# Channel mix of seven batches beside the last ticks of the second attention, and the slots' norms at later steps of the first

## The chip, the cores and the metric

The kernel runs on one core of a Trainium2 chip, as one program with one launch. The metric is the device time of one execution in microseconds (us). The engines are TensorE (PE: matmuls and transposes; its weight loads are listed as PEld), VectorE (DVE), ScalarE (ACT), GpSimd (POOL) and SyncE (SP), which issues most of the DMAs. Each engine has its own queue and takes its instructions in order; semaphores connect them.

## The reference, cut to what matters

Two layers, each an attention and a feed-forward part, over `x` of 8 batches x 256 tokens x 256 channels in float32, with a context of 8 x 256 x 192:

```python
x = x + L0_xattn(layernorm(x), ctx, mask)   # 16 heads of 16
x = x + L0_ffn(layernorm(x))                # soft mixture of 8 experts, 128 slots each
x = x + L1_xattn(layernorm(x), ctx)         # 16 heads of 64, output bias
x = x + L1_ffn(layernorm(x))                # channel mix
```

The edit touches two pieces of it. The first is the norm of the experts' slots, computed once: `sn = slots / max(|slots|, 1e-12) * 16 * gamma`, with 8 x 128 slots of 256 channels. The second is the channel mix of the last line, per batch:

```python
x_prev = concat([zeros, x[:, :-1]], axis=1)      # the token before
xr = mu_r * x + (1 - mu_r) * x_prev
xk = mu_k * x + (1 - mu_k) * x_prev
out = sigmoid(xr @ W_r.T) * (relu(xk @ W_k.T) ** 2 @ W_v.T)
```

## The kernel before, in words

All activations stay on the chip: `x_sb` holds the 16 tiles of 128 tokens (two a batch). Everything is float32. A scheduler places instructions by data dependences and may take them out of the written order, except those wrapped in `tc.keep_in_program_order`; after that every engine's queue is fixed.

**First attention** (spans about 5 to 275 us). A loop over 76 steps `h`: each does the scores of a quarter-batch twice, once by query for the row maxima (`NM`, DVE reductions, line 486) and, six steps later, once by key for the exponentials (ACT, line 497). The scores go to two PSUM buffers (`ps_big`), and a step's scores wait until the maxima of the step before have been read from them. What else is done lies in a table written out by hand, `at(h, f)`: function `f` runs at step `h`. In it are the layer-norm statistics of tile pairs (`ln_pair`, steps 0, 1, 2 for pairs 1, 2, 3), mask rows (`key_rows`), projections, and the slots' norm in three parts: `slot_sum(e)` (a square and a sum on DVE for each of 8 experts, lines 323 and 324, steps 1 to 4), `slot_scale` (one square root on ACT and three small DVE instructions, step 5), and `slot_piece(e2)` (scaling, four transposes on PE, two DVE instructions, steps 17, 25, 33, 41). The slots (`se`, 1 MB) are loaded by SP after the other inputs. The result `snT` is first read at step 48.

**Mixture of experts** (about 275 to 912 us): PE streams the experts' matmuls. The edit doesn't touch it.

**Second attention** (about 900 to 1315 us). A software pipeline over 32 groups of two steps (a step is two heads of a batch; four groups are a batch) with five stages: 0 scores, maxima (line 1201) and exponentials (line 1206, four a step); 1 the normalisation on POOL (line 1219); 2 the transposes of the weights (`pe`) with copies `et` (line 1235, one on DVE and one on ACT); 3 values (`o`); 4 the output projection (`po`, after the last group of a batch), added to `x_sb` on DVE (line 1267). Tick `n` runs stage 3 of group n-3, the next batch's projections, stage 4 of n-4, stage 2 of n-2, stage 1 of n-1, and stage 0 of n. Batch 7 is groups 28 to 31, so batch `b` is complete in `x_sb` at tick 4b+7. At n = 20 the statistics of tiles 0 to 7 for the next part are written (`ln_half`). Its matmuls and transposes are kept in program order. The PSUM pool `mm` has three buffers, used by all projections and transposes.

**Channel mix** (about 1315 us to the end). After the attention's pools are closed, the three weights and `mu` are loaded by SP (lines 1321 to 1324). `run_pipeline` then runs three stages over the eight batches: `mix` (layer norm, four transposes `pt_xf`, a copy `yT` with a zero column ahead, and for each of r and k two ACT scalings, line 1343, and two DVE instructions, line 1346), `keys` (`pk`, relu on ACT, square on POOL, line 1369; `pr`, sigmoid on ACT, line 1382), `values` (`pv`, the product on DVE, line 1398, the add of `x_sb` on POOL, line 1399, and the store).

Of the kernel before, what the change touches and what calls it, by code (L numbers as in the profile page):

```python
# [7 lines left out]

F32 = mybir.dt.float32
U8 = mybir.dt.uint8  # L10
AF = mybir.ActivationFunctionType
ALU = mybir.AluOpType
AX = mybir.AxisListType

P = 128
# [7 lines left out]
EPS = 1e-5  # L23
# [39 lines left out]
def kernel(ctx: ExitStack, tc: tile.TileContext, a: dict, out: bass.AP):  # L63
    nc = tc.nc
# [6 lines left out]
    def matmul(out, lhsT, rhs, start, stop):  # L71

        tc.keep_in_program_order(nc.tensor.matmul(out, lhsT=lhsT, rhs=rhs, start=start, stop=stop))  # L73
# [10 lines left out]
    def ps_mm(name):  # L84
        return ps.tile([P, 512], F32, tag="mm", bufs=3, name=name)
# [23 lines left out]
            a["x"][P * n : P * (n + of), :].rearrange("(t p) d -> p t d", p=P),  # L109
        )  # L110

    def ln_half(half, name):

        mv = stat.tile([P, 8, 2], F32, tag="mv", name=f"mv_{name}")
        for i in range(8):
            st = stat.tile([P, 6], F32, tag="bst", bufs=4, name=f"bst_{name}_{i}")
            nc.vector.bn_stats(st, x_sb[:, half * 8 + i, :])
            nc.vector.bn_aggr(mv[:, i, :], st)
        rstd = stat.tile([P, 8], F32, tag="rstd", name=f"rstd_{name}")
        nc.scalar.activation(rstd, mv[:, :, 1], AF.Sqrt, bias=epsb)  # L120
        nc.vector.reciprocal(rstd, rstd)
        return mv, rstd

    def ln_tiles(n, of, name):

# [10 lines left out]
    def ln_pair(p, name):  # L136
        return ln_tiles(4 * p, 4, name)
# [85 lines left out]
    with ExitStack() as l0:  # L223
# [96 lines left out]

        def slot_sum(e):
            sq = work.tile([P, 2, D], F32, tag="xh", bufs=3, name=f"sq_{e}")
            nc.vector.tensor_tensor(sq[:, 0, :], se[:, e, :], se[:, e, :], ALU.mult)
            nc.vector.tensor_reduce(ssq[:, e : e + 1], sq[:, 0, :], AX.X, ALU.add)

        def slot_scale():

            nc.scalar.activation(ssq, ssq, AF.Sqrt)
            nc.vector.tensor_scalar(ssq, ssq, 1e-12, None, ALU.max)
            nc.vector.reciprocal(ssq, ssq)  # L330
            nc.vector.tensor_scalar(ssq, ssq, 16.0, None, ALU.mult)
# [244 lines left out]
        def at(h, f):  # L576
            whole.setdefault(h, []).append(f)
# [7 lines left out]
        queries0(0, 0)  # L585
        stats0 += [ln_tiles(2, 2, "l0_1")]
        for p in range(1, 4):
            at(p - 1, lambda p=p: stats0.extend([ln_pair(p, f"l0_{2 * p}")] * 2))
        at(0, lambda: keys0(0, 1))
        at(1, lambda: queries0(0, 1))  # L590
        at(1, lambda: tokens0(1))
# [18 lines left out]
            at(h + 25, lambda b=b: values0(b + 1))  # L610

        for e in range(E):
            at(1 + e // 2, lambda e=e: slot_sum(e))
        at(5, slot_scale)
        for g in range(3):
            at(16 * g + 28, lambda g=g: moe_mean(g))
        at(30, lambda: moe_scale([0]))
        at(63, lambda: moe_scale([1, 2]))
        for e2 in range(4):
            at(17 + 8 * e2, lambda e2=e2: slot_piece(e2))  # L620
        for b in range(B):
            for qb in range(2):
                at(8 * b + 19, lambda b=b, qb=qb: project(b, qb, tos[b]))
# [438 lines left out]
    with ExitStack() as l1:  # L1062
# [15 lines left out]
        nc.sync.dma_start(wo, a["wo1"].rearrange("(c p) f -> p c f", p=P))  # L1078
        bo = w1p.tile([P, D], F32, name="bo1")
        nc.sync.dma_start(bo, a["bo1"].partition_broadcast(P))  # L1080

        def keys(p, t2):

# [196 lines left out]
        def stage(k, n):  # L1280
            for step in groups[n] if 0 <= n < len(groups) else ():
                if k < len(step):
                    step[k]()
# [6 lines left out]
        for pieces in qs:  # L1290
            for piece in pieces:
                piece()
        for n in range(len(groups) + 4):
            b, i = n // 4 + 1, n % 4
            stage(3, n - 3)
            if b < B:
                for piece in projs[b][1][i]:
                    piece()
            stage(4, n - 4)
            stage(2, n - 2)  # L1300
            stage(1, n - 1)


            if i < 2 and n // 8 < B // 2 - 1:
                keys(n // 8 + 1, n % 8 // 4 * 2 + i)()
            elif i >= 2 and b < B:
                projs[b][2][i - 2]()()
            stage(0, n)
            if n == 20:
                ffn_stats[0] = ln_half(0, "ffn_0")  # L1310

    with ExitStack() as l1f:
        wf = l1f.enter_context(tc.tile_pool(name="wf", bufs=1))
        pf_ = l1f.enter_context(tc.tile_pool(name="pf", bufs=2))
        wts = {}
        for n in ("wrT", "wkT", "wvT"):
            wts[n] = wf.tile([P, 2, D], F32, name=f"sb_{n}")  # L1320
            nc.sync.dma_start(wts[n], a[n].rearrange("(c p) f -> p c f", p=P))
        mu = wf.tile([P, 4], F32, name="mu")
        nc.sync.dma_start(mu[:, 0:2], a["mu_r"])
        nc.sync.dma_start(mu[:, 2:4], a["mu_k"])
        omu = wf.tile([P, 4], F32, name="omu")
        nc.vector.tensor_scalar(omu, mu, -1.0, 1.0, ALU.mult, ALU.add)
        ffn_stats[1] = ln_half(1, "ffn_1")

        steps = []
        for b in range(B):  # L1330
            st = {}

            def mix(b=b, st=st):
                mv, rstd = ffn_stats[b // 4]
                pt = transposed(normed(b, mv, rstd, "ffn"), f"xf_{b}")
                yT = pf_.tile([P, 2, S + 1], F32, tag="yT", name=f"yT_{b}")
                nc.gpsimd.memset(yT[:, :, 0:1], 0.0)
                nc.vector.tensor_copy(yT[:, :, 1 : S + 1], pt)
                for k, n in enumerate(("r", "k")):
                    m = pf_.tile([P, 2, S], F32, tag=f"x{n}", name=f"x{n}_{b}")  # L1340
                    for c in range(2):
                        i = 2 * k + c
                        nc.scalar.activation(
                            m[:, c, :], yT[:, c, 1 : S + 1], AF.Copy, scale=mu[:, i : i + 1]
                        )
                        nc.vector.scalar_tensor_tensor(
                            m[:, c, :],
                            yT[:, c, 0:S],
                            omu[:, i : i + 1],
                            m[:, c, :],  # L1350
                            ALU.mult,
                            ALU.add,
                        )
                    st[n] = m

            def keys(b=b, st=st):
                pk = ps_mm(f"pk_{b}")
                for d in range(2):
                    for c in range(2):
                        nc.tensor.matmul(  # L1360
                            pk[:, d * S : (d + 1) * S],
                            lhsT=wts["wkT"][:, c, d * P : (d + 1) * P],
                            rhs=st["k"][:, c, :],
                            start=(c == 0),
                            stop=(c == 1),
                        )
                ka = pf_.tile([P, 512], F32, tag="ka", name=f"ka_{b}")
                nc.scalar.activation(ka, pk, AF.Relu)
                nc.gpsimd.tensor_tensor(ka, ka, ka, ALU.mult)
                st["ka"] = ka.rearrange("p (d n) -> p d n", d=2)  # L1370
                pr = ps_mm(f"pr_{b}")
                for t in range(2):
                    for c in range(2):
                        nc.tensor.matmul(
                            pr[:, t * D : (t + 1) * D],
                            lhsT=st["r"][:, c, t * P : (t + 1) * P],
                            rhs=wts["wrT"][:, c, :],
                            start=(c == 0),
                            stop=(c == 1),
                        )  # L1380
                r = pf_.tile([P, 512], F32, tag="rs", name=f"rs_{b}")
                nc.scalar.activation(r, pr, AF.Sigmoid)
                st["rs"] = r

            def values(b=b, st=st):
                pv = ps_mm(f"pv_{b}")
                for t in range(2):
                    for d in range(2):
                        nc.tensor.matmul(
                            pv[:, t * D : (t + 1) * D],  # L1390
                            lhsT=st["ka"][:, d, t * P : (t + 1) * P],
                            rhs=wts["wvT"][:, d, :],
                            start=(d == 0),
                            stop=(d == 1),
                        )
                y = pf_.tile([P, 2, D], F32, tag="y", name=f"y_{b}")
                yf = y.rearrange("p t d -> p (t d)")
                nc.vector.tensor_tensor(yf, pv, st["rs"], ALU.mult)
                nc.gpsimd.tensor_tensor(
                    yf, yf, x_sb[:, 2 * b : 2 * b + 2, :].rearrange("p t d -> p (t d)"), ALU.add  # L1400
                )
                nc.sync.dma_start(
                    out[S * b : S * (b + 1), :].rearrange("(t p) d -> p t d", p=P), y
                )

            steps.append([mix, keys, values])
        run_pipeline(steps)


# [60 lines left out]
```

## Time and profile before

| | |
|---|---|
| median of 3 runs | 1375.91 us (1373.8 to 1378.23) |
| the profiled execution | 1375.81 us, span 1373.9 us from first to last instruction |
| busy in the span | PE 1326.6 us (97%), DVE 575.1 (42%), ACT 578.9 (42%), POOL 194.6 (14%) |
| mean granted TensorE clock | 0.987 |
| chain that ended last | PE 84%, ACT 6%, DVE 4%, DMA 2%, issue 2%, POOL 1% |

The profile is of one execution. The page gives busy time by engine, the span in 40 slices, the chain of work that ended last (followed back from the last instruction, at each step to what released it) and the costliest groups of instructions. A timeline lists instructions by start and duration; in square brackets stands the idle time of the engine just before, and what ended it. Where a row stands for several instructions (x2, x8), its time is from the first start to the last end.

### The profile page before, as it was taken

What the parts mean: (1) busy time and instruction counts of PE and PEld (TensorE: products, weight loads), DVE (VectorE), ACT (ScalarE), POOL (GpSimd) and SP (SyncE); (2) the same over time, 40 slices, a digit from 0 to 9 for tenths busy, and PEclk for the clock granted to TensorE, in tenths of its full rate; (3) what the DMA queues carried; (4) which work ended last, traced back from release to release, by engine and by line L of the source; (5) the groups of instructions that cost most, each with busy time, mean ns of one, the idle gap of its engine ahead of it and who ended that gap; (6) DMA issues with size and microseconds to landing.
All of it is one profiled execution on the core that took longest, in us unless ns stands there. A gap on an engine that the chain in (4) does not pass through costs nothing.

```text
span 1373.9 us, 19006 instructions
## 1 busy us (share of the span) xinstructions
PE 1326.6 (97%) x7504; PEld 961.3 (70%) x7504; DVE 575.1 (42%) x1172; ACT 578.9 (42%) x1386; POOL 194.6 (14%) x149
## 2 busy tenths in 40 slices
PE   6899999899999999999999999999999999999988
PEld 3556655468678877778767888866667667577767
DVE  5777876523330233321333110025444544554544
ACT  1445444635342254522625222204544534554643
POOL 1000001101010000100001000013332332323514
PEclk9899999999999999999999999999999999999999
DMA  8000000023133323332323325340000000000011
GB/s 250 23 2 1 1 1 1 1 96 131 65 131 131 131 76 119 130 113 83 126 69 130 131 88 173 100 126 1 1 1 1 1 1 1 1 1 1 1 31 54
DMA packets 59112, 86.84 MB, mean 63 GB/s; under 512 B 3344, under 2 KB 49040, under 8 KB 59024
## 3 DMA queue, kind: packets, MB, share of 16 engines
q1 hardware_dynamic: 57440, 84.33, 18.8%
q10 hardware_dynamic: 1584, 1.31, 0.4%
q8 instruction: 59, 0.97, 0.3%
q14 instruction: 29, 0.24, 0.1%
HBM read 83.53 MB, written 2.10 MB: 62 GB/s over the span
## 4 chain that ended last, share of the span: by engine, by line
PE 84%; ACT 6%; DVE 4%; DMA 2%; issue 2%; POOL 1%; SPq 0%; POOLq 0%; ACTq 0%; DVEq 0%
PE ph L964 16%; PE pe L980 15%; PE sc L73 8%; PE q L73 6%; PE o L73 5%; PE po L73 5%; PE k L73 5%; PE pc L1006 4%; PE v L73 4%; PE pe L76 4%; PE ln L828 3%; PE pf L910 3%; ACT ex L1206 2%; PE pf L73 1%; ACT ex L497 1%
## 5 line engine op out<-in xcount | busy, mean ns | idle before, releaser
L972 ACT ACTIVATE ht<-ph,b 128x256 f32<-128x256 f32 x256 | 119.0, 473 | 372.1 <-PE ph L964 371.7
L964 PE MATMUL ph<-slots,w 128*128 128x256 f32 x1024 | 266.8, 384 | 1.1 <-ACT ht L972 0.4
L980 PE MATMUL pe<-w,ht 128*128 128x256 f32 x1024 | 263.3, 381 | 0.0
L964 PEld LDWEIGHTS ph<-slots,w 128*128 128x128 f32 x1024 | 182.4, 189 | 54.4 <-ACT ht L972 21.7
L980 PEld LDWEIGHTS pe<-w,ht 128*128 128x128 f32 x1024 | 192.0, 190 | 29.9 <-DVE slots L989 4.2
L1219 POOL TENSOR_TENSOR ex<-ex,rz 128x1024 f32<-128x1024 f32 x64 | 120.2, 1898 | 224.4 <-DVE rz L1217 219.8
L1206 ACT ACTIVATE ex<-sc,nm 128x256 f32<-128x256 f32 x256 | 117.2, 483 | 45.8 <-DVE nm L1201 44.6
L73 PE MATMUL sc<-KT,QT 17*128 17x256 f32 (+1 forms) x1024 | 105.5, 383 | 5.7 <-DVE NM L486 4.8
L497 ACT ACTIVATE ex<-sc 128x512 f32<-128x512 f32 x128 | 74.6, 596 | 84.4 <-PE sc L73 76.6
L486 DVE TENSOR_REDUCE NM<-sc 128x2 f32<-128x512 f32 x128 | 86.7, 687 | 33.0 <-PE sc L73 28.7
L989 DVE TENSOR_TENSOR slots<-pe,b 128x512 f32<-128x512 f32 x32 | 22.1, 692 | 185.0 <-PE pe L980 185.0
L73 PEld LDWEIGHTS sc<-KT,QT 17*128 17x128 f32 (+1 forms) x1024 | 78.0, 189 | 29.0 <-issue 13.3
L73 PE MATMUL q<-xT,wq 128*128 128x256 f32 x384 | 95.4, 396 | 0.9 <-ACT V L1171 0.9
L73 PEld LDWEIGHTS q<-xT,wq 128*128 128x128 f32 x384 | 71.3, 193 | 27.0 <-issue 13.3
L888 POOL TENSOR_TENSOR es<-es,zs 128x1024 f32<-128x1024 f32 x12 | 22.7, 1893 | 445.8 <-DVE zs L887 445.8
L1201 DVE TENSOR_REDUCE nm<-sc 128x4 f32<-128x1024 f32 x64 | 75.4, 1219 | 6.5 <-PE sc L73 2.8
L73 PE MATMUL po<-wo,ot 128*128 128x256 f32 x320 | 72.6, 382 | 0.0
L76 PE MATMUL pe<-ident,ex 128*128 128x128 f32 x512 | 69.9, 278 | 0.5 <-DVE xT L1121 0.4
L73 PEld LDWEIGHTS po<-wo,ot 128*128 128x128 f32 x320 | 60.1, 190 | 11.3 <-issue 3.6
L1235 ACT COPY et<-pe 128x512 f32<-128x512 f32 x64 | 37.0, 607 | 71.9 <-PE pe L76 71.5
L76 PEld LDWEIGHTS pe<-ident,ex 128*128 128x128 f32 x512 | 56.3, 140 | 14.0 <-issue 8.0
L73 PE MATMUL o<-et,V 128*64 128x256 f32 x512 | 62.8, 385 | 0.9 <-ACT ot L1254 0.9
(186 smaller groups left out, 1642.7 us busy)
## 6 DMA issues: line engine op xcount, KB each, us to landing
w<-in_w_dram SPq DMA_DIRECT2D x64, 1024.0 KB, 6.4
b<-in_b_dram SPq DMA_DIRECT2D x32, 128.0 KB, 6.7
out_dram<-y SPq DMA_DIRECT2D x8, 256.0 KB, 2.1
x_sb<-in_x_dram SPq DMA_DIRECT2D x3, 512.0 KB, 6.1
ctx0T<-in_ctxT_dram SPq DMA_DIRECT2D x4, 256.0 KB, 6.8
ctx1T<-in_ctxT_dram SPq DMA_DIRECT2D x8, 128.0 KB, 5.9
se<-in_slots_dram SPq DMA_DIRECT2D x1, 1024.0 KB, 6.0
wq<-in_wq_dram SPq DMA_DIRECT2D x1, 1024.0 KB, 4.9
```

The source lines that it names most:

```text
L73: tc.keep_in_program_order(nc.tensor.matmul(out, lhsT=lhsT, rhs=rhs, start=start, stop=stop))
L76: tc.keep_in_program_order(nc.tensor.transpose(out, in_, ident))
L486: nc.vector.tensor_reduce(NMs[(2 * b + t // 2) % 2][:, qb, t, HD0 + 1 + 64 * i : 64 * i + 64 : 32], sc[i][:, :, 0, :], AX.X, ALU.max, nega ...
L497: nc.scalar.activation(ex[:, 2 - 2 * i : 4 - 2 * i, :], sc[1 - i][:, :, 1, :], AF.Exp)
L828: nc.tensor.matmul(pl[:, m * 512 : (m + 1) * 512], lhsT=st["xnT"][:, c, t * P : (t + 1) * P], rhs=snT[:, c, m * 512 : (m + 1) * 512], star ...
L964: nc.tensor.matmul(ph, lhsT=c_["w1"][:, c, hc * P : (hc + 1) * P], rhs=slots[e][:, c * 256 : (c + 1) * 256], start=(c == 0), stop=(c == 1),)
L972: nc.scalar.activation(ht, ph, AF.Gelu, bias=b1[:, e, hc : hc + 1])
L980: nc.tensor.matmul(c_["pe"][:, b, :], lhsT=c_["ht"][hc][:, b * SL : (b + 1) * SL], rhs=c_["w2"][:, hc, :], start=(hc == 0), stop=(hc == HI ...
L1006: nc.tensor.matmul(pc[:, :D], lhsT=CT[:, bl, e, t * P : (t + 1) * P], rhs=eos[e][:, bl, :], start=(e == 0), stop=(e == E - 1),)
L1201: nc.vector.tensor_reduce(nm, sc, AX.X, ALU.max, negate=True)
L1206: nc.scalar.activation(ex[:, i, qb, :], sc[:, i, qb, :], AF.Exp, bias=nm[:, i, qb : qb + 1], accum_out=z[:, i, qb : qb + 1],)
L1219: nc.gpsimd.tensor_tensor(ex, ex, rz.rearrange("p h q -> p (h q)").unsqueeze(2).to_broadcast([P, 4, S]), ALU.mult,)
```

## The change

It does four things.

1. The first attention's table: statistics of pairs 1 to 3 at steps 1 to 3, slot sums at steps 18 to 25, `slot_scale` at step 30, `slot_piece` at steps 32, 36, 40 and 44. The square and the root are kept in program order.
2. The channel mix's weights, `mu`, `omu` and one `yT` buffer move into the second attention's pool, loaded behind its own weights. The mix's other tiles take over the buffer of keys of batches 4 and 5 and the query weights `wq`, which are free by tick 28; there are two sets, for even and odd batches.
3. The pieces of batches 0 to 6 are put into a list and taken from it up to three times a tick from tick 28: after stage 3 and the projections, after stage 1, and at the end of the tick. Eighteen of the 21 pieces are taken so, in ticks 28 to 33. The statistics are computed at ticks 24, 26, 28 and 32; batch 7's follow after the last tick, and then the last pieces in the order keys 6, values 5, mix 7, values 6, keys 7, values 7. All its matmuls and transposes are kept in program order.
4. The inverse root of the mix's layer norm is computed on DVE, by an integer first guess and three Newton steps, instead of a square root on ACT. The sigmoid becomes a tanh, `sigmoid(v) = 0.5 * (1 + tanh(v / 2))`. The product and the residual add become two DVE instructions; POOL's add goes away. Batch 7's values are done and stored in two halves.

The diff, cut to its core:

```diff
-    def ln_half(half, name):
...
+    def ln_newton(pool, n, of, name):
+        mv = pool.tile([P, 4, 2], F32, tag="mvf", bufs=3, name=f"mv_{name}")
+        for i in range(of):
             st = stat.tile([P, 6], F32, tag="bst", bufs=4, name=f"bst_{name}_{i}")
+            tc.keep_in_program_order(nc.vector.bn_stats(st, x_sb[:, n + i, :]))
             nc.vector.bn_aggr(mv[:, i, :], st)
...
+        nc.vector.tensor_scalar(v, mv[:, :of, 1], EPS, None, ALU.add)
+        nc.vector.tensor_scalar(
+            t.bitcast(I32), v.bitcast(I32), 1, None, ALU.logical_shift_right
+        )
+        nc.vector.tensor_scalar(
+            y[:, :of].bitcast(I32), t.bitcast(I32), -1.0, float(0x5F3759DF), ALU.mult, ALU.add
+        )
+        for _ in range(3):
+            nc.vector.tensor_tensor(t, y[:, :of], y[:, :of], ALU.mult)
+            nc.vector.scalar_tensor_tensor(t, t, -0.5, v, ALU.mult, ALU.mult)
+            nc.vector.scalar_tensor_tensor(y[:, :of], t, 1.5, y[:, :of], ALU.add, ALU.mult)
+        return mv, y
...
-            at(p - 1, lambda p=p: stats0.extend([ln_pair(p, f"l0_{2 * p}")] * 2))
+            at(p, lambda p=p: stats0.extend([ln_pair(p, f"l0_{2 * p}")] * 2))
...
-            at(1 + e // 2, lambda e=e: slot_sum(e))
-        at(5, slot_scale)
+            at(18 + e, lambda e=e: slot_sum(e))
+        at(30, slot_scale)
...
-            at(17 + 8 * e2, lambda e2=e2: slot_piece(e2))
+            at(32 + 4 * e2, lambda e2=e2: slot_piece(e2))
...
+            KT = p1.tile([P, 8, 512], F32, tag="KT", bufs=2, name="mix_home")
+            rows = [KT[:, k, :] for k in range(8)]
+            rows += [wq.rearrange("p c (h f) -> p (c h) f", h=2)[:, k, :] for k in range(2)]
+            names = ("r", "k", "ka", "rs", "y")
+            homes.extend(dict(zip(names, rows[5 * k : 5 * k + 5])) for k in range(2))
...
-                nc.scalar.activation(r, pr, AF.Sigmoid)
+                nc.scalar.activation(st["rs"], pr, AF.Tanh, scale=0.5)
...
+                parts = ((0,), (1,)) if b == B - 1 else ((0, 1),)
+                for ts in parts:
...
+                    nc.vector.scalar_tensor_tensor(
+                        y[:, u, :], t_of[:, u, :], 1.0, pv[:, u, :], ALU.add, ALU.mult
+                    )
+                    nc.vector.scalar_tensor_tensor(
+                        y[:, u, :],
+                        y[:, u, :],
+                        0.5,
+                        x_sb[:, 2 * b + ts[0] : 2 * b + ts[-1] + 1, :],
+                        ALU.mult,
+                        ALU.add,
+                    )
+                    nc.sync.dma_start(
...
+        mixes = [channel_mix(b) for b in range(B)]
+        beside = []
+        for k in range(B + 1):
+            beside += [mixes[k - i][i] for i in range(3) if 0 <= k - i < B - 1]
+
+        def side(n):
+            if n >= 28 and len(beside) > 3:
+                beside.pop(0)()
+
+        for n in range(len(groups) + 4):
+            b, i = n // 4 + 1, n % 4
+            if n == 28:
+                homes_of_mix()
+            for at_tick, first, of in ((24, 0, 2), (26, 2, 2), (28, 4, 2), (32, 6, 1)):
+                if n == at_tick:
+                    stats_of_mix(first, of)
+            stage(3, n - 3)
+            if b < B:
+                for piece in projs[b][1][i]:
+                    piece()
+            side(n)
+            stage(4, n - 4)
+            stage(2, n - 2)
+            stage(1, n - 1)
+            side(n)
...
+            stage(0, n)
+            side(n)
+        stats_of_mix(B - 1, 1)
+
+        mix, mixed_keys, mixed_values = mixes[B - 1]
+        for piece in beside[:2] + [mix] + beside[2:] + [mixed_keys, mixed_values]:
+            piece()
```

## The prediction

> **What bounds the kernel now.** I read the page first: its slices, then its chain.
>
> ```profile
> PE   6899999899999999999999999999999999999988
> DVE  5777876523330233321333110025444544554544
> PEclk9899999999999999999999999999999999999999
> ```
>
> A slice is 34.3 us. TensorE (PE) is the bound nearly everywhere, so work moved from one stage to another gains nothing by itself; only time in which PE waits or runs at a low clock can be won. That lies at the two ends, the two places that the edit touches.
>
> The head, by the chain of the first 275 us, then by the timeline:
>
> ```profile
> 25.27 5.95 DMA se<-in_slots_dram
> 31.25 0.76 DVE sq L323 x2
> ```
>
> ```profile
> 31.25 0.76 DVE L323 TENSOR_TENSOR sq<-se 128x256 f32<-128x256 f32 x2 [3.11 <-DMA se<-in_slots_dram]
> 36.21 0.77 PE L73 MATMUL sc<-KT,QT 17*128 17x256 f32 x4 [3.36 <-DVE NM L486]
> 43.08 0.92 PE L73 MATMUL sc<-KT,QT 17*128 17x256 f32 x8
> 47.71 0.71 PE L73 MATMUL sc<-QT,KT 18*128 18x256 f32 x8
> ```
>
> VectorE (DVE) stops for 3.11 us on the slots' load, with the maxima (NM) of step 3 queued behind; then it does slot sums, statistics and mask rows without a gap until 42.8, while the scores of steps 4 and 5 wait for NM. The table of stretches shows what it costs PE:
>
> ```profile
> 30.00:33.00 3.00, 2.85 (x7) 1.69 (x5) 1.75 (x6) 0.20 (x1) 0.00 (x0) 0.50 1.02 359
> 33.00:36.00 3.00, 0.00 (x0) 0.00 (x0) 3.00 (x12) 0.39 (x2) 0.00 (x0) 0.95 1.07 361
> 39.00:42.00 3.00, 3.00 (x7) 1.54 (x6) 3.00 (x8) 0.00 (x0) 0.00 (x0) 0.50 0.02 5
> ```
>
> The columns are stretch, length, busy PE, weight loads, DVE, ACT, POOL, then granted clock: 33 to 36 has no matmul at all, and around it the clock is 0.50.
>
> The end, by the timeline:
>
> ```profile
> 1301.70 2.43 PE L73 MATMUL o<-et,V 128*64 128x256 f32 x16 [0.88 <-ACT ot L1254]
> 1307.96 7.17 PE L73 MATMUL po<-wo,ot 128*128 128x256 f32 x32
> 1320.07 0.91 ACT L1343 ACTIVATE xr<-yT,mu 128x256 f32<-128x256 f32 x2 [1.87 <-DMA mu<-in_mu_k_dram]
> 1322.04 3.75 PE L1360 MATMUL pk<-xk,sb_wkT 128*128 128x256 f32 x8 [6.04 <-DVE xk L1346]
> 1331.89 1.89 PE L1389 MATMUL pv<-sb_wvT,ka 128*128 128x256 f32 x8
> 1369.75 1.26 POOL L1399 TENSOR_TENSOR y<-y,x_sb 128x512 f32<-128x512 f32 x1 [0.46 <-DVE y L1398]
> ```
>
> Attention's last matmul ends at 1315.15. The mix's weights are only then loaded (the first at 1315.21), so PE waits 6.04 us, the first eight matmuls take 3.75 us instead of 1.73 (the chain's figure for later groups), and from 1315.15 to the end at 1373.9 are 58.75 us.
>
> **Part 1, the slots' norms.** Slot sums leave steps 1 to 4 for 18 to 25, their root leaves 5 for 30, the pieces leave 17, 25, 33, 41 for 32, 36, 40, 44, and the statistics of pairs 1 to 3 start a step later. Removed before step 6: the 3.11 us wait and eight pairs of 0.41 us instructions, which in a row cost 0.67 us a pair (two took 31.25 to 32.6): 5.4 us; DVE's queue loses 8.5 us. What is then late? On DVE, from 18.9 to step 6's scores there stood 28.8 us (18.9 to 47.7); less 8.5 and the 1.2 us for which it waited on PE at 42.8, it gets there at 38.0. On PE, from 28.8: queries 3.4 (at the clock of 0.50 that they had), scores 1.2, transposes 1.05, keys 2.5 (between 1.72 at full clock and 3.41 at 0.50), scores 0.6, keys 1.06, queries 1.94, transposes 0.6: 41.1. PE is now later; statistics that come a step later may push NM back, so I take 41.5 instead of 47.7: **6.2 us earlier** (bounds 3.1, the wait alone, and 9.7, DVE's end of it).
>
> Price of the later places: 0.67 us in each of steps 18 to 25, where DVE has idle stretches of 0.95, 1.43 and 1.21 us a step (rows at 97.2, 101.2, 107.2), except in 85 to 95, where it is busy 9.71 of 10 us; but there piece 0 (0.6 + 0.88 us) leaves. The root and three small instructions join the table load (1.28 us at 127.8) that step 30 has anyway, 0.2 to 0.7 us on the chain. Pieces in 32 to 44, where DVE is 82% busy (28.54 of 35 us), may cost 0.5 us each for the two that are new there. As much again is relieved at 17 and 25. I take 1.0 us (0 to 3). Part 1: **-5.2 us** (-9.7 to 0).
>
> **Part 2, the mix beside ticks 28 to 33.** Per batch PE does transposes 0.44, pk and pr 1.73 each, pv 1.73. From tick 28's start (1266.47) before: 107.4 us to the end. After:
> - Attention's own PE time: o 1.88, pe 2.03, sc 1.93 in ticks 28 to 31 (23.4), two po of 7.1 (14.2), and o and pe of ticks 32 to 34 (9.7): 47.3. Before took 48.7.
> - Eighteen pieces: seven mixes 3.1, six key pieces 20.8, five value pieces 8.7: 32.6.
> - After the last po, batch 7's chain: x_sb add 0.7; statistics 1.1; root by Newton, 12 dependent small instructions at 0.2 (the starts of lines 166 to 169 lie 0.2 apart) 2.4; xh 0.75; transposes 0.65, behind keys 6 and values 5 (5.2 us of PE in that time); yT 0.9; xr and xk 2.3 (1329.32 to 1331.64); pk 1.75; relu 0.85, square 1.1; first half of pv 1.1, two DVE instructions a half, 1.8; store 2.9 (POOL's last end, 1371.0, to 1373.9). Sum 18.3.
> - Stalls, unknown: 5 (below).
>
> Together 103.2, **-4.2 us**. Its covers: ACT has 5.4 us a tick now (eight exponentials of 0.45, copies 1.75) and gets four scalings 1.8, relu 0.57, tanh 0.6: 8.4. DVE has 4.1 (maxima 2.36, copies 1.37, reciprocals 0.35) and gets xh 0.73, yT 0.68, four mixes 1.75, two output instructions 1.4: 8.6. POOL 3.75 + 1.04. A tick on PE grows from 5.83 to 11.4 us, so nothing else binds by throughput. Batches 0 to 6 pay the Newton roots (2.4 us of DVE in ticks 24, 26, 28, 32) beside PE; if that cover goes, tick 28 pays up to 4.9 us, statistics and root.
>
> Stalls: three PSUM banks ("mm") now also hold pt, pk, pr and pv. In the steady tick before, ACT empties its two banks only after the exponentials (its copies at 1271.04, PE's transposes done at 1270.3), and now the second mix of tick 28 waits for them (0.8); xk of batch 0 queues behind the same exponentials (0.5); yT has one buffer for two batches (0.7). Two us there. Then DVE against POOL:
>
> ```profile
> 1337.05 1.68 DVE L1346 SCALAR_TENSOR_TENSOR xk<-yT,omu,xk 128x256 f32<-128x256 f32 x2
> 1337.41 1.04 POOL L1369 TENSOR_TENSOR ka<-ka 128x512 f32<-128x512 f32 x1 [1.55 <-ACT ka L1368]
> 1347.05 0.88 DVE L1346 SCALAR_TENSOR_TENSOR xr<-yT,omu,xr 128x256 f32<-128x256 f32 x2 [0.65 <-ACT xr L1343]
> ```
>
> The pair of instructions takes 1.68 us beside POOL and 0.88 without. POOL's 1.9 us normalisations will now run beside them: I add 0.6 us in each of five ticks, 3 us. Range of stalls 1.4 (today's) to 12. A rule speaks against the change here: the Trainium skill, SBUF — State Buffer, Terms, says of the port pair that DVE and GpSimd share that the loser "fully blocks". By it the stalls would go to their upper end, 12, and the sum to 1373.4; by the row they stay at 5.
>
> Tanh: no row shows one. Bounds: no table load, or two of 1.28 us a batch, ACT then 11.0 of 11.4 us. Relu and Copy run between the Sigmoids without a load; I take none, and leave the other for the range. The skill's ScalarE: Activation LUTs, Table sets, puts tanh in exp's set, which would give the same sum.
>
> Queues: SP issues the five small loads behind bo at 905, with nothing behind them until the stores. POOL loses eight adds (1.27) and seven memsets; the square of ka may queue behind two normalisations (3.75), and only pv, one tick later, waits for it. At no cost.
>
> Sum: -5.2 - 4.2 = -9.4 us on the profiled 1375.81 us (span 1373.9 and 1.9 around it; the runs' median is 1375.91): **1366.4 us**.
>
> **The rivals.** (a) *The stalls eat the end*: 9.5 us in ticks 28 to 33 leave Part 1 alone, 1371. For it: ACT and DVE in order, three banks; against: PE work of 11 us a tick. (b) *The head is bound elsewhere*: PE stays at a clock of 0.50 and NM waits for the later statistics; Part 1 gives 1, total 1370.5. (c) *Both at their good ends*, 1.5 us of stalls and 8 us at the head: 1360. (d) *Slower, DVE becomes the bound of the ticks*: if POOL's instructions (two of 1.9, one of 1.04) held it for their whole length, where the row shows 0.8 of 1.04, 8.6 and 4.8 us make 13.4 against 11.4, 2 us in each of six ticks; with tick 28's 4.9 us and its two more, 19 us of stalls, 9.8 us lost at the end; with 3 us from the head, 1382. It decides once DVE, blocked time included, passes 11.4 us a tick.
>
> **How the numbers follow.** Forecast (1362 to 1370) 0.58, (a) 0.15, (b) 0.11, (c) 0.09, (d) 0.07. 0.3%, about what a measurement here can tell from no change, is 4.1 us: faster is below 1371.8, same reaches to 1380. Faster holds the forecast, (c), most of (b) and about a third of (a): 0.82; same the rest of (a) and an edge of (b): 0.11; slower (d): 0.07. The range takes in (a), (b) and (c), and goes 2 us past (c) and 3 past (a), since the bounds of the head (9.7) and of the stalls (12) lie beyond them: 1358 to 1374.
>
> **What would show it.** Right: no wait of DVE on se near 28, scores of step 6 at 41 to 42, no PE gap after the last po above 2 us, 18 to 19 us from that po to the end, ticks of 11.5 to 12.5 us, no table load near a tanh. Wrong: PE waits on DVE xk, ACT ka or et in ticks 28 to 33 above 9 us, pairs of table loads there, or stalls in steps 18 to 44 as long as the head's gain.

## The result and the profile after

After: **1385.04 us** median of 4 runs (1383.65 to 1389.04), before on the same chip 1375.16 us; ratio 1.0073, 95% interval 1.0045 to 1.0102. The change makes the kernel slower by 0.7%, where 1366.4 us was forecast and the range ended at 1374. The profiled execution took 1389.04 us (span 1387.3), 13.4 us more in span than before's. It is the longest of the four; the medians differ by 9.9 us.

The page of after, busy tenths in slices of 34.7 us:

```profile
PE   7998999899999999999999999999999999989898
DVE  5687776623330233321333110025543534466764
POOL 1000001001010000100101000013332422332420
```

In slices 36 to 39 DVE has risen from 5454 to 6676, with POOL at 2 to 4 beside it. That is the mix under the attention. In these last five slices PE has 8 in slices 36, 38 and 40, where before had it in 39 and 40 only: it waits in the stretch that was meant to fill it.

To place the loss, the same matmuls were paired in both traces. The table gives the start in after less the start in before, and in the last column what each stretch adds to it:

| place (time in before) | difference, us | change there |
|---|---|---|
| first scores (18.1) | +1.26 | +1.3 |
| scores after the head (50.9) | -4.93 | **-6.2** |
| scores before step 30 (121.2) | -3.68 | +1.25 |
| scores of step 48 (180.0) | +3.55 | **+7.2** |
| po of batch 4 (1209.3) | +4.00 | +0.45 (+2.0 by 290, -1.6 near 1180) |
| first values of tick 28 (1266.4) | +9.61 | **+5.6** |
| end (1373.9) | +13.4 | **+3.8** |

The head, by the timeline of after (the lines answer to those at 31.25 to 47.71):

```profile
32.23 0.71 PE L74 MATMUL sc<-KT,QT 17*128 17x256 f32 x8
35.52 0.67 DVE L503 TENSOR_REDUCE NM<-sc 128x2 f32<-128x512 f32 x1
36.24 1.36 PE L74 MATMUL sc<-KT,QT 17*128 17x256 f32 x8 [1.00 <-DVE NM L503]
42.60 0.71 PE L74 MATMUL sc<-QT,KT 18*128 18x256 f32 x8
```

No DVE wait on `se` is left, PE's 3.36 us wait is 1.00, and the scores of step 6 start at 42.60 instead of 47.71. Counted from the first scores to 50.9, that is the 6.2 us forecast.

Step 30, by the timeline of after:

```profile
125.42 0.21 ACT L345 ACTIVATE ssq<-ssq 128x8 f32<-128x8 f32 x1
126.34 0.63 DVE L182 TENSOR_SCALAR scl<-scl 128x4 f32<-128x4 f32 x1
126.89 0.34 DVE L354 TENSOR_SCALAR sn<-se,ssq 128x256 f32<-128x256 f32 x1
127.55 0.61 DVE L354 TENSOR_SCALAR sn<-se,ssq 128x256 f32<-128x256 f32 x2
128.07 1.28 DVE L503 TENSOR_REDUCE NM<-sc 128x2 f32<-128x512 f32 x2
129.44 0.71 PE L74 MATMUL sc<-QT,KT 18*128 18x256 f32 x8 [1.82 <-ACT ex L514]
130.52 1.07 PE L77 MATMUL nm<-ident,NM 128*128 128x128 f32 x4
```

The root is followed by four scalings `sn` of pieces 32 and 36, which the scheduler has taken ahead of the step's maxima (presumably because DVE would otherwise idle for a moment; the trace doesn't show the reason). The maxima, the exponentials behind them and then PE come late: a wait of 1.82 us where before has 0.96. One microsecond after PE resumes, `nm` takes 1.07 us for four matmuls instead of 0.66: the granted clock has fallen. The table of stretches says so (columns as in the prediction's table of stretches; before has 1.00 in both):

```profile
128.00:132.00 4.00, 2.56 (x23) 2.21 (x24) 3.03 (x7) 2.46 (x4) 0.00 (x0) 0.82 0.00 0
132.00:136.00 4.00, 3.80 (x27) 2.58 (x25) 3.32 (x10) 1.18 (x2) 0.00 (x0) 0.75 0.00 0
```

The same happens 35 us later, with the normalised rows of the routing (`xh_moe`, hoisted from steps 47 and 59) ahead of the maxima:

```profile
161.49 1.37 DVE L192 TENSOR_SCALAR xh_moe<-x_sb,mvp_moe,scl 128x256 f32<-128x256 f32 x4
162.78 1.28 DVE L503 TENSOR_REDUCE NM<-sc 128x2 f32<-128x512 f32 x2
164.15 0.72 PE L74 MATMUL sc<-QT,KT 18*128 18x256 f32 x8 [1.71 <-ACT ex L514]
```

Before had the four rows in two pairs, 22 us apart (one is at 160.88), and no wait.

Ticks 24 and 25, by the timeline of after:

```profile
1232.21 0.66 PE L77 MATMUL pe<-ident,ex 128*128 128x128 f32 x4 [0.97 <-ACT et L1264]
1232.63 0.16 DVE L134 TENSOR_TENSOR t_ffn<-rstd_ffn 128x4 f32<-128x4 f32 x1
1232.72 3.74 POOL L1248 TENSOR_TENSOR ex<-ex,rz 128x1024 f32<-128x1024 f32 x2 [6.12 <-DVE rstd_ffn L130]
1232.83 1.80 DVE L135 SCALAR_TENSOR_TENSOR t_ffn<-t_ffn,v_ffn 128x4 f32<-128x4 f32 x1
1234.66 1.82 DVE L136 SCALAR_TENSOR_TENSOR rstd_ffn<-t_ffn,rstd_ffn 128x4 f32<-128x4 f32 x1
1237.19 1.22 DVE L1230 TENSOR_REDUCE nm<-sc 128x4 f32<-128x1024 f32 x1
1238.50 0.47 ACT L1235 ACTIVATE ex<-sc,nm 128x256 f32<-128x256 f32 x1 [4.95 <-DVE t_ffn L135]
1241.96 1.16 PE L77 MATMUL pe<-ident,ex 128*128 128x128 f32 x8 [2.49 <-DVE QT L1170]
1243.06 3.54 PE L74 MATMUL sc<-KT,QT 64*128 64x256 f32 x16
```

The Newton root's instructions work on 128x4 numbers and take 0.16 us, as the one at 1232.63 does. The next two take 1.80 and 1.82 us, since normalisations now run on POOL: each lasts about as long as one of POOL's two. Behind them in DVE's queue is `nm`; ACT idles 4.95 us until it is there (the view names line 135, but `ex` reads `nm`, which ends at 1238.41). A chain of copies later PE waits 2.49 us and does the next scores at half clock (3.54 us for 2.00). These two make 4.2 of the 5.6 us lost in these ticks. The other 1.4 come before the root's first instruction (1232.02): PE waits 0.33 and 0.97 us for copies among which the statistics of four tiles stand.

The second root, written at tick 26, is blocked in the same way, and costs nearly nothing:

```profile
1253.22 1.75 DVE L135 SCALAR_TENSOR_TENSOR t_ffn<-t_ffn,v_ffn 128x4 f32<-128x4 f32 x1
1255.00 1.82 DVE L136 SCALAR_TENSOR_TENSOR rstd_ffn<-t_ffn,rstd_ffn 128x4 f32<-128x4 f32 x1
1260.00 0.47 ACT L1235 ACTIVATE ex<-sc,nm 128x256 f32<-128x256 f32 x1 [4.01 <-DVE nm L1230]
1262.47 7.07 PE L74 MATMUL po<-wo,ot 128*128 128x256 f32 x32
```

The exponentials are late again, by 4.01 us, but PE has `q` and `po` in front of it (1258.91 to 1269.54), and ticks 26 and 27 lose under 0.2 us. So a blocked root costs only where PE soon needs what stands behind it.

The end, ticks 28 and 29 of after:

```profile
1282.93 0.66 PE L77 MATMUL pt_xf<-ident,xh_ffn 128*128 128x128 f32 x4 [1.63 <-ACT et L1264]
1285.97 2.06 DVE L192 TENSOR_SCALAR xh_ffn<-x_sb,mv_ffn,rstd_ffn 128x256 f32<-128x256 f32 x1
1288.03 1.21 DVE L1230 TENSOR_REDUCE nm<-sc 128x4 f32<-128x1024 f32 x1
1294.81 2.82 PE L77 MATMUL pe<-ident,ex 128*128 128x128 f32 x12 [2.29 <-ACT mix_home L1390]
```

The first line is the wait for a PSUM buffer (a bank) that was foreseen for tick 28's second mix (0.8 forecast, 1.63 measured; in experiment 3, whose tick 28 has neither statistics nor root, no wait in it is above 0.3 us). The second is again a DVE instruction blocked by POOL (0.41 us alone), with the maxima `nm` behind it; the exponentials, relu and tanh then crowd ACT, and PE waits 2.29 us for a bank that the tanh empties. From tick 28 to the last po are 91.8 us, 11.9 more than the 79.9 us of PE work that were summed; from there to the end 19.5.

One stretch got shorter without being forecast, near 1180 (-1.6 us). There before has, at tick 20, the statistics and square root of `ln_half`, with two table loads on ACT (1167.54 and 1173.31), and scalings `xh_ffn` on DVE ahead of the maxima (2.10 us for two, beside POOL). The exponentials and the copies behind them are late, and PE waits:

```profile
1173.31 1.28 ACT L1206 ACT_TABLE_LOAD   x1 [3.07 <-DVE nm L1201]
1179.37 1.13 PE L73 MATMUL k<-ctx0T,wk 128*128 128x512 f32 x2 [1.71 <-ACT et L1235]
```

After has no `ln_half` there and waits 1.06 us. All kernels below with the mix inside the attention win the same 1.6 us; `part1`, `head2` and `head3`, which keep `ln_half`, don't.

### The profile page after: what moved, and what is told of

Read it like the earlier page. It is cut to its first block, busy times and chain, and to the rows that moved or that the text cites. A ratio compares the mean times of both kernels' runs of the same rounds, so it can differ in the third digit from the quotient of the medians.

```text
span 1387.3 us, 19035 instructions
## 1 busy us (share of the span) xinstructions
PE 1333.3 (96%) x7504; PEld 961.7 (69%) x7504; DVE 598.6 (43%) x1240; ACT 573.4 (41%) x1380; POOL 183.9 (13%) x134
## 4 chain that ended last, share of the span: by engine, by line
PE 82%; DVE 9%; ACT 7%; issue 1%; DMA 1%; POOL 0%; SPq 0%; ACTq 0%; POOLq 0%; DVEq 0%
PE ph L981 16%; PE pe L997 15%; PE sc L74 7%; PE q L74 6%; PE po L74 5%; PE k L74 4%; PE o L74 4%; PE pc L1023 4%; PE v L74 4%; PE pe L77 3%; PE ln L845 3%; PE pf L927 3%; ACT ex L1235 2%; DVE NM L503 1%; ACT ex L514 1%; PE pf L74 1%
## 5 line engine op out<-in xcount | busy, mean ns | idle before, releaser
L981 PEld LDWEIGHTS ph<-slots,w 128*128 128x128 f32 x1024 | 182.3, 189 | 54.5 <-ACT ht L989 21.8
L77 PEld LDWEIGHTS pe<-ident,ex 128*128 128x128 f32 x512 | 57.5, 143 | 20.1 <-issue 10.2
```

Of the source, the lines that this page charges most:

```text
L77: tc.keep_in_program_order(nc.tensor.transpose(out, in_, ident))
L981: nc.tensor.matmul(ph, lhsT=c_["w1"][:, c, hc * P : (hc + 1) * P], rhs=slots[e][:, c * 256 : (c + 1) * 256], start=(c == 0), stop=(c == 1),)
```

## The experiments

Times are medians, with ratios to before measured on the same chip. "Offset" is the difference of a matmul's start against before in the profiled executions.

**1. Only the slots' norms** (`part1`: before with the table of after, square and root kept in order).

```
at(p, ... ln_pair)              # was p - 1
at(18 + e, ... slot_sum(e))     # was 1 + e // 2
at(30, slot_scale)              # was 5
at(32 + 4 * e2, ... slot_piece) # was 17 + 8 * e2
```

> The kernel before with only the slots' norms moved. Theory of the later places: the head gains 4.9 us at step 6, and the sums in 18 to 25 cost 1.2, root and pieces in 30 to 44 cost 7.2, routing 2.0 as in the trace of after: 3 to 6 us slower than before, about 1380. Rival (the prediction's sum for Part 1, the 7 us being noise of the clock in one execution): 4 to 5 us faster, 1371. If the loss of steps 30 to 44 needs the end's code in some way, the time is at or below before.

Measured: 1377.75 us, ratio 1.0023 (1.0014 to 1.0032). The offset goes from -0.5 at the first scores to -6.7 at 50.9 (6.2 won, as in after), to -5.4 at 121 and to +3.5 at 180: 9.0 us lost in steps 30 to 48, with the same two waits (1.82 and 1.70 us) and the clock at half behind both. The later places alone turn the gain of the head into a loss, of 2.8 us by the medians (3 to 6 expected).

**2. Only the mix beside the ticks** (`part2`: after with before's table and order).

> The change with the slots' norms where they were before; only the mix beside the last ticks. Theory (ticks 24 to 27 lose 5.6 us to the Newton roots, the end loses 3.8): 6 to 9 us slower than before, 1382 to 1385; ticks 24 to 26 lose the same 5 to 6 us against before. Rival (the end suffers only because it comes at another place after a changed head, or the profiled run of after was an unlucky one): 0 to 4 us faster, 1372 to 1376.

Measured: 1381.32 us, ratio 1.0049 (1.0032 to 1.0065). Ticks 24 to 27 lose 5.6 us (offset -4.18 to +1.43), tick 28 to the end takes 111.7 us (107.5 before). The excesses of the two halves over before, 2.8 and 6.3 us, add to 9.1 of the 9.9 of the whole change: within the scatter they simply add. The head of this kernel is that of before, and yet it takes 2.1 us less in this execution (offset +0.43 to -1.66): a gain of the head read from one pair of traces is uncertain by about that much.

**3. Roots during the projections** (`root_po`: after, statistics and Newton root written ahead of stage 4).

```
for at_tick, first, of in ((19, 0, 2), (23, 2, 2), (27, 4, 1), (31, 5, 1)):
    if n == at_tick:
        stats_of_mix(first, of)
stage(4, n - 4)     # was: ahead of stage 3, ticks 24, 26, 28; tick 32 stays
```

> The change with the statistics and the Newton roots of batches 0 to 5 written just before the projections (po) in ticks 19, 23, 27 and 31, where GpSimd is idle, instead of in ticks 24, 26 and 28. Theory (each tiny instruction of the root takes 1.8 us in place of 0.16 because a 1.89 us normalisation of GpSimd runs beside it): the tiny instructions take 0.2 us each, ticks 24 to 26 lose nothing against before, and the kernel is 5 to 7 us faster than after, 1378 to 1380. Rival 1 (the ticks lose because DVE has too much work, 4 to 5 us more, wherever it stands): the 5 us are lost in ticks 20 to 27 all the same, total within 1.5 us of after. Rival 2 (the statistics themselves, not the root): the loss moves to ticks 20 and 24, 2 to 3 us are won.

Measured: 1376.58 us, ratio 1.0016 (1.0006 to 1.0026), 8.5 us better than after by the medians, where 5 to 7 were expected. The timeline shows the same instructions during `po`, with POOL idle:

```profile
1210.66 7.07 PE L74 MATMUL po<-wo,ot 128*128 128x256 f32 x32
1214.54 0.16 DVE L135 SCALAR_TENSOR_TENSOR t_ffn<-t_ffn,v_ffn 128x4 f32<-128x4 f32 x1
1214.73 0.16 DVE L136 SCALAR_TENSOR_TENSOR rstd_ffn<-t_ffn,rstd_ffn 128x4 f32<-128x4 f32 x1
```

The offset stays at +1.33 from 1187 to 1266, so ticks 20 to 27 lose nothing (5.6 us won), and tick 28 to the end falls from 111.3 to 108.5 us. The work is the same but for one root more (batches 4 and 5 have one each), so both rivals fall: at these places neither the amount of DVE's work nor the statistics cost PE time. Two things differ, though: no normalisation runs beside the roots, and PE has 7 us of `po` to do meanwhile. The durations show the first; the tick 26 of after, above, shows that the second alone is enough.

**4. sn in program order** (`sn_kept`: after with `tc.keep_in_program_order` around the `sn` multiplications).

> The change with the multiplications of the normalised slots (sn) kept at their place in the program's order, so that they can't go ahead of a step's maxima. Theory (at step 30 root and sn ahead of the maxima delay the scores by 1.8 us, and a clock of 0.50 for 3 us follows): steps 30 to 36 lose 1.5 to 3 us less than after, total 1381 to 1383.5. Rival (the pieces cost by their own PE work and waits, whatever their order, or the root alone makes the delay): within 1 us of after, 1385.

Measured: 1381.83 us, ratio 1.0056 (1.0034 to 1.0078). The median is within the theory, but the trace doesn't show why: at step 30 the wait is 1.30 us instead of 1.82 and half clock follows all the same (10.2 us of it), and a new wait of 1.99 us stands ahead of a piece's transposes at 175. By itself inconclusive; runs 9 to 12 go on from it.

**5. Pieces at other steps** (`pieces_free`: `at((33, 38, 41, 46)[e2], ...)`).

> The change with the four slot pieces at steps 33, 38, 41 and 46 (steps without keys, tokens, queries or a projection) instead of 32, 36, 40, 44. Theory (the pieces cost because they meet the additions of keys and the tokens' norms on DVE, and xh_moe then goes ahead of the maxima): of the 4 to 5 us that steps 32 to 44 lose in after, 2 to 4 are won, total 1381 to 1383. Rival (the multiplications by VectorE that are hoisted ahead of a step's maxima do it, wherever the pieces stand): within 1 us of after, 1385.

Measured: 1381.32 us, ratio 1.0053 (1.0038 to 1.0068). From 141 to 180 the offset goes from +0.72 to +1.65, 0.9 us instead of the 4.4 of after; the 1.7 us wait behind `xh_moe` is gone. The median is in the theory's range. Step 30 is unmended: its wait of 1.83 us is followed by 13.65 us at half clock, 6.7 us lost by 141.

**6. xh_moe in program order** (`xm_kept`: kept at steps 47 and 59).

> The change with the routing's normalised rows (xh_moe of batches 0 and 1) kept at their place in the program's order, at steps 47 and 59, so that the four of them (1.37 us) can't stand ahead of the maxima of step 41 or so. Theory: the PE wait of 1.70 us near 161 to 164 and the 3.4 us at half clock behind it go, 2.5 to 4 us; step 47 pays up to 1.5 us for rows that now come just in time: total 1382 to 1384. Rival (some other work takes the gap in DVE's queue, or the wait is that of the piece itself): 1385, the wait stays above 1.2 us.

Measured: 1383.53 us, ratio 1.0071 (1.0054 to 1.0088). The wait near 160 falls to 0.41 us and 141 to 180 loses 1.5 us, as the theory has it; step 59 gets a wait of 1.20 us on `xh_moe`. In the median 1.5 us are won against after, at the edge of what the intervals can tell.

**7. Two pieces a tick** (`spread`: root_po with pieces taken from tick 27 on, at the first and last of the three places).

> root_po (1376.6) with two pieces of the mix a tick from tick 27 on (at the first and the last of the three places of a tick) instead of three a tick from tick 28 to 33. Theory (the stalls of ticks 28 to 33 come from too many PSUM and ScalarE demands in one tick: two mixes in tick 28, key pieces and exponentials on ScalarE): the waits of 2.2, 1.0 and 0.9 us shrink, stalls fall by 3 to 5 us, total 1372 to 1374. Rival (the waits come of the order of ScalarE's queue in any tick with a key piece, 0.9 us each): within 1 us of root_po. Rival 2 (ticks 34 and 35, with little attention left, gain less cover than batch 7's chain loses): 1 to 2 us slower.

Measured: 1379.18 us, ratio 1.0034 (1.0022 to 1.0046), 2.6 us worse than root_po. The waits of ticks 28 to 31 do vanish (gaps from tick 28 to the last po 4.15 us against 6.50), but in tick 33, behind batch 6's root (which is still at tick 32, beside POOL: 1.84 and 1.82 us), waits of 1.36 and 1.29 us stand together, and 6.83 us at half clock follow. Tick 28 to the end is 108.5 us in both: 2.3 us less up to the last po, 2.3 us more behind it (21.8 for 19.4). Tick 27, which now holds a piece, is 1.0 us longer. So the sign is that of the second rival, by moving work behind the last po; the rest of the difference in the medians was not traced. The theory missed by 5 us.

**8. All three** (`best`: roots, pieces, two a tick).

> All three edits together: roots during the projections, two pieces of the mix a tick from 27, slot pieces at 33, 38, 41, 46. If they add: root_po less 2 to 4 (pieces) less 3 to 5 (spread): 1368 to 1371, 0.3 to 0.5% faster than before. If only the roots matter: 1376.

Measured: 1370.71 us, ratio 0.9976 (0.9963 to 0.9989), the first version below before. The expectation is met, but not by its parts: root_po less the 3.7 us that pieces_free won, plus the 2.6 that spread lost, would be 1375.5. Some 5 us of it are luck or unexplained. Tick 28 to the end is 105.9 us, with the same two waits in tick 33 as in spread and no half clock behind them in this execution. Step 30 is still the worst place; here are the stretches of best from it on:

```profile
122.00:125.60 3.60, 1.92 (x8) 1.37 (x8) 3.58 (x16) 2.60 (x6) 0.64 (x1) 1.00 0.00 0
125.60:130.00 4.40, 4.25 (x32) 3.13 (x36) 2.83 (x7) 2.51 (x5) 0.00 (x0) 0.56 0.00 0
130.00:134.00 4.00, 4.00 (x24) 2.70 (x16) 1.61 (x3) 1.23 (x3) 0.00 (x0) 0.50 0.00 0
134.00:138.00 4.00, 4.00 (x30) 2.10 (x32) 3.00 (x7) 1.52 (x4) 0.00 (x0) 0.50 0.02 4
```

**9, 10. DVE's part of the slots' root behind the maxima, sn kept** (`best2`, on best; `head2`, before with only the slots' norms at these places).

```
at(30, slot_scale)      # the root on ACT only
at(31, slot_inverse)    # maximum, reciprocal, scale; kept in program order
if n == 33: stats_of_mix(6, 1)    # best2 only, was 32
```

> best (1370.7) with three small edits more: VectorE's part of the slots' root (maximum, reciprocal, scale) kept at step 31, behind the maxima of step 30, and sn kept at its place, so that neither stands ahead of a step's maxima; and batch 6's Newton root at tick 33, behind GpSimd's last normalisation, instead of tick 32. Theory (the 1.8 us wait at step 30 and the half clock behind it come of these instructions; the two waits of 1.3 us in tick 32 come of tiny instructions of the root blocked for 1.83 and 1.82 us): the wait at step 30 is below 1.2 us as in before (0.96) with 0 to 3.4 us at half clock in place of 13.7, the two waits in tick 32 vanish; 3 to 7 us won, 1364 to 1368. Rival (the table loads at step 30 hold the exponentials all the same; the work of tick 32 is late anyway): 1370.

> The kernel before with only the slots' norms, at best2's places (sums in 18 to 25, root at 30 with VectorE's part at 31, pieces at 33, 38, 41, 46, sn kept); the channel mix stays behind the attention. If the head's gain is kept (5 to 8 us of it, less 1.2 for the sums and about 1 for root and pieces): 1369 to 1371, faster than before by 4 to 6. best2 less head2 is then what the mix beside the ticks is worth once roots and places are mended: 2 to 4 us by the sums of the trace of best (105.9 us from tick 28 to the end, 107.5 before). Rival (half the head's gain is the clock and goes into other steps): 1373 to 1375.

Measured: best2 1377.22 us, ratio 1.0009 (0.9998 to 1.002); head2 1377.92 us, 1.0023 (1.0013 to 1.0034); best2 misses its theory by 9 us and head2 its own by 7. Step 30 is mended: its wait is 1.05 us, the clock stays at 1.00, and the scores behind it lose 0.1 us. The waits in tick 33 only shrink (1.48 and 0.88 us in place of 1.36, 1.29 and 0.95): with the root gone, POOL's normalisation holds the next DVE instruction with two SBUF inputs, the residual add of line 1419, for 2.25 us instead of 0.69. And sn kept costs more than that, since it then comes after the maxima, and the piece's transposes, next in PE's queue, wait for it:

```profile
148.63 1.44 DVE L507 TENSOR_REDUCE NM<-sc 128x2 f32<-128x512 f32 x2 [1.43 <-PE sc L74]
149.99 0.61 DVE L357 TENSOR_SCALAR sn<-se,ssq 128x256 f32<-128x256 f32 x2
150.39 0.81 PE L77 MATMUL pt_sn<-ident,sn 128*128 128x128 f32 x4 [1.79 <-DVE sn L357]
```

**11, 12. The same without keeping sn** (`best3`, `head3`).

> best2 without keeping sn at its place: sn may again stand ahead of maxima, but of step 31's and not of step 30's, where the table loads are. By best2's trace, sn kept cost two waits of 1.79 us of PE on sn (steps 38 and 46) and the clock behind the second; by best's trace, pieces whose sn is early cost 0.9 us in steps 34 to 48. Theory (places and order of the small instructions, not the slots' work, make the loss): steps 30 to 48 lose 1 to 3 us in place of 7 to 9, total 1365 to 1368, 0.5 to 0.7% faster than before. Rival (the wait moves to step 31, where four sn of 0.31 us stand ahead of the maxima, and the half clock follows it there): 1370 to 1373.

> The kernel before with only the slots' norms, at best3's places and order. Theory: head 5.5 to 8 us won, 1.25 lost in steps 18 to 25, 1 to 3 in steps 30 to 48: 1369 to 1373. If best3 is 2 to 4 us below this, the mix beside the ticks with its roots during the projections is worth what is left of the predicted 4.2; if they are equal, the mix beside the ticks is worth nothing even so. Rival as for best3: 1374 to 1376.

Measured: best3 **1370.49 us**, ratio 0.9962 (0.9947 to 0.9977); head3 1372.06 us, 0.998 (0.9971 to 0.9989). Both beat before, best3 beats both kernels. Steps 30 to 48 lose 1.7 us in both (offsets -4.77 to -3.05 and -6.49 to -4.77), where part1 lost 9.0 with the same instructions; the scores behind step 30's maxima in best3:

```profile
127.59 0.71 PE L74 MATMUL sc<-QT,KT 18*128 18x256 f32 x8 [1.06 <-ACT ex L516]
```

In the first attention best and best3 differ in the place of the root's DVE part alone: from 121 to 141 best loses 6.7 us, best3 0.7. The medians of the two are equal all the same (1370.71 and 1370.49). Best's profiled execution makes it up elsewhere: 0.9 us ahead of the first scores, 1.7 in the head, and 3.2 between 180 and 290, where it has no half clock and best3 has 10.2 us of it.

best3 was forecast at 1365 to 1368 and missed that by 2.5 us. Its time is the rival's, its mechanism the theory's: at step 31 a wait of 1.05 us does appear, but no half clock follows. Against head3 it wins 1.6 us in the medians, with intervals that overlap. The two profiled spans are equal (1368.9 and 1368.8) because head3's head gained 7.8 us and best3's 6.2. From 50.9 on best3 is 1.65 us shorter: it wins 1.6 at tick 20, where it has no `ln_half`, and 0.25 from there to the end, and loses 0.2 on the way to tick 20. What the mix beside the ticks is worth by itself, once mended, is thus close to nothing in these two traces.

## Why the prediction was wrong, step by step

Part 1, forecast at -5.2 us, costs 2.8 us by itself (part1); Part 2, forecast at -4.2, costs 6.3 (part2).

- **Head, 6.2 us earlier**: right in mechanism and about right in size. After and part1 gain 6.2 us between the first scores and 50.9; the other kernels with this table 6.1 or 7.8. That the number is met to the tenth is luck: part2 with before's own head is 2.1 us faster there than before. By the medians, head3's 2.4 us plus the 1.25 and 1.7 us that it loses later make 5.4, an estimate.
- **Later places, 1.0 us (0 to 3)**: the first step that failed. The sums cost 1.25 us in every kernel with the later places, within the range given. Root and pieces cost 7.2 in after and 9.0 in part1. They were priced by their own length against DVE's idle share ("0.2 to 0.7 us on the chain", "0.5 us each"). What decides is what the scheduler takes ahead of a step's maxima, since PE has no second step's scores to go on with. Runs 9 to 12 show it for step 30: with the root's DVE part behind the maxima, and the pieces at other steps, the same work costs 1.7 us (best3 and head3). And 1.7 to 1.8 us of waiting cost more than themselves, through the clock, which the sum had no term for. This is the sign of being wrong that the prediction named last: stalls in steps 18 to 44 as long as the head's gain.
- **Newton roots of batches 0 to 6 at nothing, beside PE**: the second failure, 5.6 us in ticks 24 and 25, ahead of the stretch that was summed; 1.4 of it belong to the statistics. The condition was written down ("if that cover goes, tick 28 pays up to 4.9 us") and put in the wrong place: DVE's queue has `nm` behind the root in tick 24 as well, and PE lives on `nm` within a tick. At tick 26 the cover held, by `po`, and the root cost nothing, as forecast.
- **0.6 us a tick for DVE beside POOL**: the mechanism was seen in the rows at 1337.05 and sized wrongly. There POOL's instruction is 1.04 us long and held DVE for 0.8; its normalisations are 1.9 us, and in tick 24 each held one DVE instruction for about 1.65 (1.80 less 0.16). The size of the DVE instruction doesn't matter, so twelve tiny instructions in a row are a bad thing to put there: one of them is in the queue whenever POOL starts. The rule that was weighed and set aside (the Trainium skill, SBUF — State Buffer, Terms: the loser "fully blocks") was the better price. The same page, under Who interferes with whom, limits it to DVE instructions with two SBUF inputs or in a two-port mode; the traces agree as far as they go: in the second attention of after, line 135 (two SBUF inputs) takes 0.15 us alone and 1.79 beside POOL, while the maxima `nm`, which read PSUM, take 1.21 and 1.22.
- **Stalls of 5 us in ticks 28 to 33** (bounds 1.4 to 12): 11.9 in after, the bad end: 7.7 us of PE gaps, 1.7 for 3.41 us at half clock, and the remaining 2.5 in PE's own busy time, which was summed too small (82.8 us in root_po, at full clock throughout, for 79.9). With roots moved and two pieces a tick the gaps are 4.5 (best).
- **18.3 us after the last po**: 19.5. In it PE waits 1.66 us for `xk`, whose DVE instructions stand among the outputs of batches 5 and 6.
- **`ln_half` at tick 20**: its removal wins 1.6 us that the sum had no term for, in the change's favour.
- Tanh, the weights' loads and the square of `ka`: after's last table load is at 948.7 and its first tanh at 1294.2, and no wait on these loads was found, as forecast.

Rival (d) had the mechanism of the larger half, DVE held by POOL for whole instructions, and 1382 us, at a chance of 0.07. It was priced low because throughput was compared (13.4 us of DVE against 11.4 of PE a tick); the loss comes from order within a tick and starts four ticks before those it counted.

## What to carry to other kernels

Price a small instruction that is moved onto an in-order queue by what stands behind it there and who waits for that, not by its length or the engine's idle share. Put chains of tiny VectorE instructions where GpSimd is idle, or where the tensor engine has several us of work that doesn't depend on what stands behind them. In a kernel whose tensor engine is 97% busy a wait has a second price: here, above some 1.2 us within 3.41 us, it could take the clock with it, so that two short waits in one place can be worse than two apart.

## What the runs showed of the hardware

**Half clock comes in fixed pieces.** In all 14 traces every stretch of 0.50 granted clock inside the kernel is 3.41 us long or a whole multiple (6.83, 10.24, 13.65), and within a trace all of them start on one grid of 3.413 us, whose phase differs from execution to execution. Cutting the traces (41 us to some 1350) by that grid: of some 5,170 full-clock pieces in which PE was busy for 65% or more, none was followed by half clock; of 17 with less than 45%, 16 were; in between, 48 of 77. So a wait of 1.2 to 1.9 us is enough if it falls into one piece, and costs up to 1.7 us more for each piece (3.41 us at half speed); the same wait of 1.41 us between 55 and 66 was followed by half clock in 13 of 14 traces and not in root_po's. The Trainium skill, TensorE: Matmul & The Clock Gate, Part 1, gives the free-running window of 3413 ns, with which this agrees, and an idle window of about 3.4 us as the condition. Of the 64 pieces with half clock behind them, PE was idle throughout in three (from 1316.7 in before, 1319.9 in head2, 1311.7 in head3, where it waits for the mix's weights); in the others it was busy for 25% of the piece or more. Here less than an idle window is enough. The fixed pieces fit part of the scatter of the runs of one kernel (0.7 to 7.6 us here): the head's gain takes two values, 6.1 to 6.2 and 7.8 us, and they differ by what one piece costs.

**A kept order can cost as much as a free one.** Keeping `sn` at its place cost 5.9 us (head2 less head3), through two PE waits of 1.79 us and the half clock behind the second.

Not explained: part of spread's median, and the 5 us by which best is below the sum of its parts.
